# A kernel of four graph layers: the attention of layer 2 transposed by VectorE's blocks and DRAM, and work of VectorE and GpSimd put at other times

## The chip, the core and the metric

The kernel runs on one core of a Trainium2 chip. Its engines are TensorE (PE in the profile, its weight loads are PEld), VectorE (DVE), ScalarE (ACT), GpSimd (POOL) and SyncE (SP), which issues the DMAs. The metric is the device time of one execution in microseconds. All data are float32.

## The reference

`x` has 128 graphs of 128 nodes with 512 features. `adj` is one 128 x 128 matrix for all graphs. Four layers follow one another, each with a residual and a layer norm over the features:

```python
def _L0_gnn_ref(x, adj, weight, bias):
    y = jnp.einsum('nm,bmd->bnd', adj, x)
    return jnp.einsum('bnd,do->bno', y, weight) + bias

def _L1_gnn_ref(s, adjacency, Wq, Wk, Wv):
    q, k, v = s @ Wq.T, s @ Wk.T, s @ Wv.T            # shortened
    rel = adjacency.T[None, :, :] * jnp.einsum('bnd,bmd->bnm', q, k)
    rel = rel / jnp.linalg.norm(rel, axis=2, keepdims=True)
    return jnp.einsum('bnm,bmd->bnd', rel, v)

def _L2_gnn_ref(x, W, a, beta, mask):
    h = jnp.einsum('bnc,cf->bnf', x, W)
    s1, s2 = h @ a[:F_, 0], h @ a[F_:, 0]             # shortened
    e = leaky_relu(s1[:, :, None] + s2[:, None, :], negative_slope=0.2) * mask
    att = jax.nn.softmax(e, axis=2)
    h_prime = jnp.einsum('bij,bjf->bif', att, h)
    return jax.nn.elu(h_prime + beta * h)

def _L3_gnn_ref(x, W1, W2, b):
    A = jnp.einsum('od,bdn->bon', W1, x)
    C = jnp.einsum('od,bdn->bon', W2, x) + b[None, :, None]
    return jnp.max(relu(A[:, :, None, :] + (C - A)[:, :, :, None]), axis=-1)

x = _layernorm(x + _L0_gnn_ref(x, adj, L0_gnn_weight, L0_gnn_bias))
x = _layernorm(x + _L1_gnn_ref(x, adj, L1_gnn_Wq, L1_gnn_Wk, L1_gnn_Wv))
x = _layernorm(x + _L2_gnn_ref(x, L2_gnn_W, L2_gnn_a, L2_gnn_beta, adj))
x = _layernorm(x + _L3_gnn_ref(x, adj, adj, L3_gnn_b))
```

The change is about layer 2. The kernel computes `(att + beta I) x W`: it needs the matrix `att + beta I` transposed, with the nodes that are summed over on the partitions.

## The kernel before

The graphs go through in 32 groups of four (G = 4, NG = 32). Each engine runs its instructions in program order and waits on semaphores for the data. The program order comes from a table of slots: `emit(at, f)` notes a piece of work with its slot, and all pieces are emitted in the order of their slots. A group advances by 28 slots, so slot 65.8 of one group stands beside slot 9.8 of the group two later. The slots set only the order on each engine; nothing holds an instruction back to the time of its slot.

```python
TABLE = dict(
    load=[-20], y=row(0.5, 1), bias=row(1.3, 1), y_sums=row(5.2, 0.5), y_w=row(7, 1, 7),
    ...
    spread=[61.6], leaky=[62.0], weighted=[63.4], greatest=[64.3], exps=[64.4],
    divide=[65.8], turn_att=[68.6], with_beta=[69.0], gather=row(71.5, 1),
    z_sums=row(75.3, 0.5), z_w=row(77, 1, 7), exp=[87.5, 88.5, 90.4, 92.0],
    elu=[87.8, 89.4, 92.8, 93.8], norm2=[95.0], apply2=row(95.7, 0.33),
    widen=[98.7, 100.0, 103.6, 104.6], top=[99.1, 100.4, 104.0, 105.0],
    stats3=[99.8, 101.1, 104.7, 105.7], norm3=[106.2], apply3=row(107, 0.33), store=[108.5],
)
```

The four large products of a group (y_w, m, v, z_w; layer 0's and 2's weights, and layer 1's scores and values) are each split into seven block products with sums of blocks. The sums of the left factor are made by GpSimd (`left_factors`: s1, s2, s3, s4; s2 needs s1, s4 needs s2). The seven products run in the order 1, 2, 6, 5, 7, 3, 4, a slot apart, in accumulators in PSUM: one of two buffers r0 for 1, 6, 7, 4, and a single buffer r12 for first 2 and then 5 and 3. Each is evicted 0.72 slots after it is emitted; in the y product VectorE does all seven evictions. Product 6 takes s2, product 5 s1, product 7 s3, product 3 s4.

```python
r[where] = psum.tile([P, 2, H], FP, tag="r0" if where == 0 else "r12",
                     name=f"r{where}_{name}", bufs=2 if where == 0 else 1)
...
for n, i in enumerate(ORDER):
    emit(at[n], step, i)
    emit(at[n] + 0.72, out, i)
```

The attention of layer 2, for four graphs at once (e is 128 x 4 x 128):

```python
def leaky():                                   # VectorE, twice
    e = work.tile([P, G, P], FP, tag="e", name=f"e_{g}")
    dve.tensor_tensor(e, s["p"]..., s12[g]..., ALU.add)
    dve.scalar_tensor_tensor(e, e, ALPHA, e, op0=ALU.mult, op1=ALU.max)
def weighted():
    pool.tensor_tensor(s["e"], s["e"], adj_b, ALU.mult)
def greatest():
    dve.tensor_reduce(s["nm"], s["e"], AX.X, ALU.max, negate=True)
def exps(i):                                   # ScalarE, four times, with the sums of the rows
    ...
def divide(i):
    rs = small.tile([P, n], FP, tag=f"rs{n}", name=f"rs_{g}_{i}")
    dve.reciprocal(rs, s["sums"][:, i * n : i * n + n])
    e = s["e"][:, i * n : i * n + n, :]
    engine = pool if n == G else dve
    engine.tensor_tensor(e, e, rs[:, :, None].to_broadcast([P, n, P]), ALU.mult)
def turn_att(i):
    for b in range(i * n, i * n + n):
        pe.transpose(s["p"][:, b * P : (b + 1) * P], s["e"][:, b, :], ident)
def with_beta(i):                              # out of PSUM, with beta on the diagonal
    dve.tensor_tensor(s["eT"]..., s["p"]..., beta_b..., ALU.add)
def gather(b):                                 # z = (att + beta I) x, transposed
    pe.matmul(p[:, k * P : (k + 1) * P], x2[g][:, b, k * P : (k + 1) * P], s["eT"][:, b, :], ...)
```

Layer 0's bias is added to the residual by GpSimd, one graph at a time (`biased`), in place. elu is two VectorE operations and the statistics of the norm; layer 3 is one matmul (`widen`) and a maximum (`top`) for each graph. At the end of layer 1 VectorE makes two dot products of each graph with a vector (`dots`) and three tiny operations on their 4 x 2 results (`scale`). Layer 1's x and rel are already transposed without TensorE in most groups: VectorE transposes blocks of 32 x 32, and DMAs move the blocks. The last three groups have tables of their own (LAST).

## Time and profile before

| | before |
|---|---|
| time, median of 3 runs | 2218.94 us (2217.63 to 2219.58) |
| span of the profiled execution | 2214.6 us |
| TensorE granted clock, mean | 0.996 of full speed |
| DVE busy | 1547.9 us (70%) |
| ACT busy | 1102.5 us (50%) |
| POOL busy | 907.7 us (41%) |
| DMA moved | 115.15 MB |
| transposes of e on TensorE | 128, 273 ns each |
| with_beta on VectorE, 128x512 | 31, 674 ns each |
| multiply by 1/sum on GpSimd, 128x512 | 31, 1049 ns each |

The profile is one execution. The page gives each engine's busy time and the chain of work that ended last, followed back from the last instruction to what released each step. A row of the order of time has the start and the duration in us, the engine, the operation, what it writes and reads with the shapes, and the count of instructions merged in the row; in brackets it has the engine's idle time before it and the operation whose end released it. Matmuls overlap, so that a TensorE instruction's duration is longer than its share of the engine's time: the distance of two starts tells more.

### The profile page before, as it was taken

How to read it: one execution, taken by the hardware profiler on the slowest of the kernel's cores; microseconds unless marked ns; L12 is line 12 of the kernel's file. 1: busy time of each engine (PE TensorE's matmuls, PEld its weight loads, DVE VectorE, ACT ScalarE, POOL GpSimd, SP SyncE). 2: the span in 40 equal slices, each digit the busy share in tenths (PEclk: the TensorE clock that was granted, in tenths of full speed). 3: DMA queues.
4: the chain of work that ended last, by engine and by line, in shares of the span. 5: the costliest groups of instructions: out<-in, count | busy, mean ns of one | idle time of the engine just before them, and what ended most of it. 6: DMA issues, size and time to landing. Idle time of an engine off the chain costs nothing.

```text
span 2214.6 us, 31863 instructions
## 1 busy us (share of the span) xinstructions
PE 2170.9 (98%) x11073; PEld 1839.6 (83%) x11073; DVE 1547.9 (70%) x3290; ACT 1102.5 (50%) x2446; POOL 907.7 (41%) x743
## 2 busy tenths in 40 slices
PE   7999999999999999999999999999999999999996
PEld 5788888888888888888888888888888888888873
DVE  4657766767766767776767776767767677667676
ACT  2224445554445554445554445554455554455547
POOL 3334444334444344443344443344443344443321
PEclk9999999999999999999999999999999999999998
DMA  4011222211222211222112222112222112221101
GB/s 167 25 20 29 61 60 62 62 20 49 60 60 63 58 21 52 59 61 62 44 31 56 58 62 63 41 30 59 58 62 63 29 39 62 59 63 44 21 28 57
DMA packets 333295, 115.15 MB, mean 52 GB/s; under 512 B 297424, under 2 KB 297552, under 8 KB 333136
## 3 DMA queue, kind: packets, MB, share of 16 engines
q1 hardware_dynamic: 331936, 110.77, 19.7%
q10 hardware_dynamic: 1200, 2.36, 0.3%
q8 instruction: 88, 1.44, 0.3%
q14 instruction: 71, 0.58, 0.1%
HBM read 39.65 MB, written 33.55 MB: 33 GB/s over the span
## 4 chain that ended last, share of the span: by engine, by line
PE 93%; DVE 3%; ACT 2%; POOL 1%; issue 1%; DMA 0%; ACTq 0%; DVEq 0%; POOLq 0%
PE r_y L26 17%; PE r_v L26 17%; PE r_m L26 17%; PE r_z L26 17%; PE p_z L26 5%; PE p_rel L26 5%; PE p_y L26 5%; PE p_o L26 5%; PE p_a L26 5%; DVE x L26 1%; ACT x L26 1%; DVE st L26 1%; PE p_eT L26 1%; PE p_m L26 1%; PE p_s L26 1%
## 5 line engine op out<-in xcount | busy, mean ns | idle before, releaser
L26 ACT ACTIVATE x<-x,nmean,rstd 128x512 f32<-128x512 f32 x384 | 288.6, 808 | 120.8 <-DVE nmean L26 120.8
L26 DVE BATCH_NORM_STATS2 st<-x 128x6 f32<-128x512 f32 x384 | 263.8, 687 | 8.8
L26 POOL TENSOR_TENSOR x<-x,bias_sb 128x512 f32<-128x512 f32 x128 | 170.1, 1331 | 137.9 <-PE p_y L26 137.5
L26 DVE SCALAR_TENSOR_TENSOR x<-m,x 128x512 f32<-128x512 f32 x128 | 114.4, 894 | 108.5 <-ACT m L26 98.5
L26 POOL TENSOR_TENSOR s_x<-xT 128x512 f32<-128x512 f32 x64 | 82.2, 1285 | 261.1 <-DMA xT<-xB 250.2
L26 ACT COPY c<-r_z 128x512 f32<-128x512 f32 x124 | 71.2, 574 | 223.3 <-PE r_z L26 198.0
L26 ACT COPY yT<-p_y 128x512 f32<-128x512 f32 x128 | 75.1, 586 | 213.6 <-PE p_y L26 213.6
L26 POOL TENSOR_TENSOR rstd<-ve,mhalf 128x4 f32<-128x4 f32 (+1 forms) x99 | 98.5, 995 | 194.1 <-DVE ve L26 188.9
L26 DVE TENSOR_TENSOR x<-r_y,x 128x512 f32<-128x512 f32 x224 | 151.7, 678 | 31.2 <-PE r_y L26 31.0
L26 DVE SCALAR_TENSOR_TENSOR scr<-x,wa 128x512 f32<-128x512 f32 x256 | 161.5, 675 | 0.0
L26 DVE STREAM_TRANSPOSE xB<-x 128x512 f32<-128x512 f32 x120 | 81.2, 696 | 108.7 <-ACT x L26 97.7
L26 PEld LDWEIGHTS p_y<-adjT,x 128*128 128x128 f32 x1024 | 136.9, 196 | 11.2 <-ACT adjT L26 4.8
L26 POOL TENSOR_TENSOR s_z<-zT 128x512 f32<-128x512 f32 x31 | 39.4, 1270 | 255.9 <-ACT zT L26 255.9
L26 PE MATMUL p_y<-adjT,x 128*128 128x128 f32 x1024 | 137.6, 280 | 4.5 <-ACT adjT L26 4.5
L26 PEld LDWEIGHTS p_z<-eT,x 128*128 128x128 f32 x1024 | 134.0, 192 | 7.9 <-issue 1.0
L26 PEld LDWEIGHTS p_rel<-xT,tT 128*128 128x128 f32 x1024 | 134.1, 191 | 7.4 <-DVE tT L26 0.8
L26 DVE TENSOR_REDUCE mx<-p_a 128x1 f32<-128x512 f32 x128 | 88.3, 691 | 69.6 <-PE p_a L26 69.6
L26 PE MATMUL p_a<-x,adjT 128*128 128x512 f32 x256 | 130.8, 596 | 5.8 <-DVE mx L26 4.4
L26 ACT COPY tT<-r_m 128x512 f32<-128x512 f32 x128 | 75.6, 590 | 121.6 <-PE r_m L26 121.6
L26 PE MATMUL p_rel<-xT,tT 128*128 128x128 f32 x1024 | 134.9, 275 | 0.6 <-DVE tT L26 0.6
L26 PE MATMUL p_z<-eT,x 128*128 128x128 f32 x1024 | 134.7, 275 | 0.1
L26 PE MATMUL p_o<-v,relT 128*128 128x512 f32 x256 | 130.4, 593 | 0.3 <-ACT v L26 0.3
(129 smaller groups left out, 5268.6 us busy)
## 6 DMA issues: line engine op xcount, KB each, us to landing
out_dram<-x SPq DMA_DIRECT2D x128, 256.0 KB, 2.5
x<-in_x_dram SPq DMA_DIRECT2D x31, 1024.0 KB, 5.3
xT<-xB SPq DMA_DIRECT2D x480, 64.0 KB, 2.3
relT<-relB SPq DMA_DIRECT2D x512, 16.0 KB, 1.8
w_sb<-in_L_gnn_weight_dram ACTq DMA_DIRECT2D x1, 1024.0 KB, 5.6
x<-in_x_dram SPq DMA_DIRECT2D x4, 256.0 KB, 7.8
wq_sb<-in_L_gnn_Wq_dram SPq DMA_DIRECT2D x1, 1024.0 KB, 12.3
wk_sb<-in_L_gnn_Wk_dram SPq DMA_DIRECT2D x1, 1024.0 KB, 15.1
```

The source lines that it names most:

```text
L26: return lambda *args, **kw: self.tc.keep_in_program_order(op(*args, **kw))
```

## The change

In all groups but the last two, `att + beta I` is transposed without TensorE. VectorE scales each graph's e by 1/sum and adds beta on the diagonal in one operation, four times, and then transposes the 32 x 32 blocks. One DMA writes the result to a DRAM scratch, and four read it back with the blocks in their places. This takes the four transposes from TensorE, the evacuation of their PSUM bank from VectorE, and the multiply from GpSimd. Besides, the order of other work is changed: the biases of graphs 2 and 3 follow layer 0's first two sums, layer 2's softmax starts a little earlier, elu of graphs 0 and 1 comes earlier and of graphs 2 and 3 later, and layer 3's four matmuls stand together.

```diff
+    dram = ctx.enter_context(tc.tile_pool(name="dram", bufs=2, space=bass.MemoryType.DRAM))
...
-        load=[-20], y=row(0.5, 1), bias=row(1.3, 1), y_sums=row(5.2, 0.5), y_w=row(7, 1, 7),
+        load=[-20], y=row(0.5, 1), bias=[4.1, 4.6, 9.1, 9.6],
+        y_sums=[6.8, 7.35, 10.2, 10.75], y_w=row(7, 1, 7),
...
-        spread=[61.6], leaky=[62.0], weighted=[63.4], greatest=[64.3], exps=[64.4],
-        divide=[65.8], turn_att=[68.6], with_beta=[69.0], gather=row(71.5, 1),
-        z_sums=row(75.3, 0.5), z_w=row(77, 1, 7), exp=[87.5, 88.5, 90.4, 92.0],
-        elu=[87.8, 89.4, 92.8, 93.8], norm2=[95.0], apply2=row(95.7, 0.33),
-        widen=[98.7, 100.0, 103.6, 104.6], top=[99.1, 100.4, 104.0, 105.0],
-        stats3=[99.8, 101.1, 104.7, 105.7], norm3=[106.2], apply3=row(107, 0.33), store=[108.5],
+        spread=[61.6], leaky=[61.6], weighted=[62.3], greatest=[63.0], exps=[63.1],
+        divide=[64.2], turn_att=[68.6], with_beta=[69.0], turn_blocks_2=[64.8], move_2=[64.9], gather=row(71.5, 1),
+        z_sums=row(75.3, 0.5), z_w=row(77, 1, 7), exp=[86.0, 87.0, 96.0, 99.6],
+        elu=[86.4, 87.4, 96.8, 100.3], norm2=[101.4], apply2=row(102.4, 0.33),
+        widen=[104.2, 104.9, 105.6, 106.3], top=[104.7, 105.4, 106.1, 106.8],
+        norm3=[107.4], apply3=row(108.4, 0.33), store=[109.8],
...
-    FIRST = {0: dict(turn=row(20.4, 0.3)), 1: dict(y=row(-9.5, 0.3), bias=row(-9.2, 0.3))}
+    FIRST = {0: dict(turn=row(20.4, 0.3)), 1: dict(y=row(-9.5, 0.3))}
...
+        late = g >= NG - 2
...
         def divide(i):
             rs = small.tile([P, n], FP, tag=f"rs{n}", name=f"rs_{g}_{i}")
             dve.reciprocal(rs, s["sums"][:, i * n : i * n + n])
+            if not late:
+                for b in range(G):
+                    e = s["e"][:, b, :]
+                    dve.scalar_tensor_tensor(
+                        e, e, rs[:, b : b + 1], beta_i, op0=ALU.mult, op1=ALU.add
+                    )
+                return
...
+        def turn_blocks():
+            s["eB"] = work.tile([P, Q, G, P // Q], FP, tag="eB", name=f"eB_{g}")
+            dve.transpose(
+                s["eB"].rearrange("p q b u -> p b q u"),
+                s["e"].rearrange("p b (q u) -> p b q u", q=Q),
+            )
+
+        def move():
+            m = P // Q
+            blocks = dram.tile([P, Q, G * m], FP, tag="eB", name=f"eBd_{g}")
+            sync.dma_start(blocks, s["eB"].rearrange("p q b u -> p q (b u)"))
+            eT = work.tile([P, Q, G, m], FP, tag="eT", name=f"eT_{g}")
+            for q in range(Q):
+                sync.dma_start(
+                    eT[q * m : (q + 1) * m].rearrange("p a b u -> p a (b u)"),
+                    blocks.rearrange("(a j) q n -> q j a n", a=Q)[q],
+                )
+            s["eT"] = eT.rearrange("p a b u -> p b a u")
...
-        each(t["turn_att"], turn_att)
-        each(t["with_beta"], with_beta)
+        if late:
+            each(t["turn_att"], turn_att)
+            each(t["with_beta"], with_beta)
+        else:
+            emit(t["turn_blocks_2"][0], turn_blocks)
+            emit(t["move_2"][0], move)
```

## The prediction

> **What bounds the kernel now.** I read the page's totals and its chain first, to see whether one engine sets the end; then TensorE's idle time by releaser, and where it lies; then the order of time within one group of four graphs, engine by engine.

> ```profile
> PE 2170.9 (98%) x11073; PEld 1839.6 (83%) x11073; DVE 1547.9 (70%) x3290; ACT 1102.5 (50%) x2446; POOL 907.7 (41%) x743
> ...
> PE 93%; DVE 3%; ACT 2%; POOL 1%; issue 1%; DMA 0%; ACTq 0%; DVEq 0%; POOLq 0%
> ```

> TensorE is busy for 98% of the span and makes 93% of the chain. Its named waits lie in the first 130 us and the last 105 us; between them there is one, of 0.4 us near 857 us. So a group costs what TensorE takes for it: the r_m product that begins a group recurs every 66.81 us (1117.92 to 1184.73 in the chain). Anything taken from TensorE shortens the kernel, and any new wait of TensorE lengthens it, 30 times over. The other engines have slack on average, but an average says nothing of one moment. So the change must be placed in the order of time.

> The four transposes that the change removes, in the order of time (start, duration, engine, operation, count):

> ```profile
> 1135.48 1.60 PEld L26 LDWEIGHTS r_y<-w_sb,s_y 128*128 128x128 f32 x8
> ...
> 1137.10 0.58 PEld L26 LDWEIGHTS p_eT<-ident,e 128*128 128x128 f32 x4
> ...
> 1137.64 1.60 PEld L26 LDWEIGHTS r_y<-t,yT 128*128 128x128 f32 x8
> ...
> 1139.27 1.70 PEld L26 LDWEIGHTS r_v<-wvT,xT 128*128 128x128 f32 x8
> ```

> They take 0.54 us (1137.10 to 1137.64), but a product behind a 128-wide group starts after 1.62 to 1.63 us instead of the 1.72 of two products in a row, so the net cost is about 0.45 us.

> [...] The trace of before [...] shows that each instruction pays anew:

> ```profile
> 107.87 3.70 POOL L26 TENSOR_TENSOR x<-x,bias_sb 128x512 f32<-128x512 f32 x3
> ...
> 107.91 2.46 DVE L26 SCALAR_TENSOR_TENSOR d<-mv,wa_sum,d 128x4 f32<-128x4 f32 x2
> ...
> 110.47 1.12 DVE L26 TENSOR_TENSOR d<-d,rstd 128x8 f32<-128x8 f32 x1
> ...
> 111.52 0.68 DVE L26 TENSOR_TENSOR tT<-r_m,tT 128x512 f32<-128x512 f32 x1
> ...
> 112.25 2.97 PE L26 MATMUL r_m<-s_x,m_qk 128*128 128x256 f32 x8 [4.39 <-DVE tT L26]
> ```

> Three GpSimd sums run back to back (3.70 us, 1.23 each, not slowed). Beside them three tiny VectorE instructions, some 0.15 to 0.2 us each when alone, take 3.6 us: one gets in after each sum. The eviction behind them (tT) is late, and TensorE waits 4.39 us. [...] behind the 4.39 us the granted clock was 0.62 over 112.2 to 116.0, behind a wait of 2.00 us at 56.70 it stayed 1.00. [...] no line of before has a round trip through DRAM.

> **The change part by part.**

> *TensorE.* In 30 of 32 groups (all but the last two) the four transposes go: 30 x 0.45 = 13.5 us less, if nothing new waits. All else on TensorE is only moved.

> *The DMA route.* The turn is ready some ten slots of the table before its use in gather: one write and four reads, each some 0.65 us to issue (16 DMAs of relT in 10.49 us) and about 2 us to land (1.8 to 2.5 in the page's DMA part): 0.65 + 2.5 + 4 x 0.65 + 2.5, about 8 us. From turn_blocks_2 at slot 8.8 to gather at 15.5 TensorE has some 16 us. An estimate, but hidden with room.

> *VectorE and GpSimd around the softmax: the part that decides.* The scale by 1/sum was one GpSimd multiply. It becomes four VectorE scalar_tensor_tensor of 128x128 with e and beta_i, both in SBUF. GpSimd's order was bias x4, y_sums x4, weighted; it becomes bias x2, weighted, y_sums x2, bias x2, y_sums x2. GpSimd works in order and starts what is ready: behind "weighted" six operations are all ready. So it runs seven in a row. The chain of e in before, to be counted from the first VectorE operation on it (call that moment L, here 1124.17):

> ```profile
> 1124.17 0.68 DVE L26 TENSOR_TENSOR e<-p_s,d 128x512 f32<-128x512 f32 x1
> ...
> 1125.74 1.27 POOL L26 TENSOR_TENSOR e<-e,adj_sb 128x512 f32<-128x512 f32 x1 [0.63 <-DVE e L26]
> ...
> 1127.04 0.69 DVE L26 TENSOR_REDUCE nm<-e 128x4 f32<-128x512 f32 x1 [0.78 <-POOL e L26]
> ...
> 1127.76 0.40 ACT L26 ACTIVATE e<-e,nm 128x128 f32<-128x128 f32 x1 [3.06 <-DVE nm L26]
> ...
> 1129.22 0.19 ACT L26 ACTIVATION_READ_ACCUMULATOR e<-e,nm 128x1 f32 x1
> ```

> The exponentials end at L + 5.24. The reciprocal and a dependent start after it (dependent small operations follow each other by 0.2 us) put the first multiply at about L + 5.47. GpSimd's pace is seen in z_sums, where the second depends on the first and the others do not:

> ```profile
> 1020.64 1.27 POOL L26 TENSOR_TENSOR s_z<-zT 128x512 f32<-128x512 f32 x1 [7.94 <-ACT zT L26]
> ...
> 1021.99 1.27 POOL L26 TENSOR_TENSOR s_z<-s_z,zT 128x512 f32<-128x512 f32 x1
> ...
> 1023.22 1.28 POOL L26 TENSOR_TENSOR zT<-zT 128x512 f32<-128x512 f32 x1
> ...
> 1024.45 1.28 POOL L26 TENSOR_TENSOR s_z<-zT,s_z 128x512 f32<-128x512 f32 x1
> ```

> Weighted starts at L + 1.57, so s1 at 2.80 (+1.23), s2 at 4.16 (+1.36), the third bias at 5.39, then 6.62, 7.85, 9.08. The third bias is thus ahead of the first multiply by 0.08 us. In before a tiny operation waiting behind a sum got in some 1.12 us after the sum's start (1110.15 to about 1111.27). So the multiplies get in near 6.51, 7.75, 9.0 and 10.25. Next in VectorE's order is the eviction of the second y product (slot 8.72 behind divide at 8.2), which ends 0.8 us later, at L + 11.05.

> TensorE needs that eviction, since the r12 accumulator has one buffer and the fourth y product (i = 5) takes it anew:

> ```profile
> 1121.22 0.60 PE L26 MATMUL p_s<-ident,d 128*128 128x128 f32 x4
> ...
> 1127.73 1.89 PE L26 MATMUL r_y<-t,s_y 128*128 128x256 f32 x8
> ...
> 1130.35 1.89 PE L26 MATMUL r_y<-w_sb,s_y 128*128 128x256 f32 x8
> ```

> In the changed kernel leaky stands directly behind spread, so L is the end of p_s, 1121.86 on this scale, and the fourth product would start at 1130.35 = L + 8.49. It has to wait to L + 11.05: 2.55 us. That is below the 4.39 us that lost clock. The third product needs s2 (ready L + 5.45, wanted near L + 5.8): just in time.

> *The rest of the moves.* elu 0 and 1 come earlier, 2 and 3 later, the four widen of layer 3 stand together before attend. I added VectorE's and ScalarE's durations by slot: both engines finish the evictions of v some 0.3 to 1.0 us before TensorE needs the bank again, and the pairs of banks for widen and attend come round in time. I count nothing for this, with up to 0.3 us a group as a risk.

> *The start.* The biases of group 1 go from slot 18.8 to 32.1 and half of group 0's behind its first sums. The waits on GpSimd's s_y (0.68 us) and s_x (2.00 us at 56.70[...]) go, and of the three tiny operations at 107.91 one no longer meets a bias (0.95): about -3 us.

> *Sum.* 30 x (2.55 - 0.45) - 3 = +60 us: 2218.9 + 60 = 2279. I place the prediction a little lower, at 2276, for the first rival.

> **The rivals.** (1) The first multiply is ahead of the third bias. The gap is 0.08 us on sums of a dozen durations, so this is nearly even. Then three waits remain, the stall is 2.55 - 1.24 = 1.3 us, and the time 2219 + 30 x 0.86 - 3 = 2242. (2) The table is meant to leave GpSimd free between 7.9 and 9.1, just where the multiplies stand. If something I don't see holds the third bias back to slot 9.1, nothing collides and only the transposes count: 2219 - 13.5 - 3 = 2202. Against it: the biases' only inputs are the load and the y matmuls, done by then, and in before GpSimd ran each bias as soon as its matmuls ended, whatever the table said. (3) More than I count: elu 2 before the last y eviction delays the v evictions[...], 0.3 to 1 us a group, 2285 to 2305. (4) The DRAM round trip is late and gather waits; that needs it to double, for which no landing of before speaks.

> **Range and chances.** About half of my weight on 2265 to 2290, a quarter on rival 1 (2230 to 2262), 14% on rival 2, a tenth above 2290. A range of 2225 to 2300 holds some 8 in 10. The 2% lines are 2174.6 and 2263.3: faster 0.01, within 0.36, slower 0.63.

> **What would show it.** Right: the multiplies e<-e,rs,beta_i at more than 1 us each, one behind each GpSimd operation; a TensorE wait of r_y on DVE x of 2 to 2.7 us in each of 30 groups, at the fourth y product; a group of about 68.9 us; no wait of p_z on a DMA. Wrong: multiplies of 0.2 to 0.3 us with GpSimd idle beside them and a group of 66.4 us (rival 2); three slow multiplies and 67.7 us (rival 1); TensorE waiting for v or eT instead (rivals 3 and 4).

## The result, and the profile after

The changed kernel takes 2319.90 us (median of 4 runs, 2317.82 to 2320.61) against 2218.28 us before: a ratio of 1.0456 (95% interval 1.0438 to 1.0475), 101.6 us more. The prediction had the direction and the wait, but not the size: 2276 us, and a range that ended at 2300.

The page's totals and its chain, of after:

```profile
PE 2202.7 (95%) x10953; PEld 1854.6 (80%) x10953; DVE 1660.9 (72%) x3410; ACT 1097.0 (47%) x2446; POOL 867.0 (37%) x713
PE 79%; DVE 12%; ACT 4%; issue 2%; POOL 2%; SPq 0%; DMA 0%; ACTq 0%; DVEq 0%; POOLq 0%
```

TensorE's share of the chain fell from 93% to 79%, and VectorE's rose from 3% to 12%: work that lay beside TensorE now lies between its products. VectorE's own busy time rose by 113 us, though the same instructions add only 28 us where the multiplies meet no GpSimd work (1575.5 us in e1, below). TensorE runs 120 transposes fewer and yet is busy for 32 us longer; a row further down shows the main part of it. The page's groups name the two operations (count | busy us, mean ns | idle time before and its releaser):

```profile
L26 PE MATMUL r_y<-w_sb,s_y 128*128 128x256 f32 x512 | 143.7, 430 | 76.6 <-DVE x L26 76.6
...
L26 DVE SCALAR_TENSOR_TENSOR e<-e,rs,beta_i 128x128 f32<-128x128 f32 x120 | 153.7, 1338 | 1.1
```

The multiply by 1/sum takes 1338 ns for 128 elements a partition, and a y product waits 76.6 us in all for VectorE (30 waits). One group in the order of time, of after, with rows left out:

```profile
1100.28 0.60 PE L26 MATMUL p_s<-ident,d 128*128 128x128 f32 x4
...
1100.92 0.69 DVE L26 TENSOR_TENSOR e<-p_s,d 128x512 f32<-128x512 f32 x1 [1.40 <-PE p_s L26]
...
1102.42 1.27 POOL L26 TENSOR_TENSOR e<-e,adj_sb 128x512 f32<-128x512 f32 x1 [9.03 <-DVE e L26]
...
1105.91 0.19 ACT L26 ACTIVATION_READ_ACCUMULATOR e<-e,nm 128x1 f32 x1
1106.13 0.18 DVE L26 RECIPROCAL rs<-sums 128x4 f32<-128x4 f32 x1 [1.06 <-ACT e L26]
1106.23 2.54 POOL L26 TENSOR_TENSOR x<-x,bias_sb 128x512 f32<-128x512 f32 x2
1106.34 5.11 DVE L26 SCALAR_TENSOR_TENSOR e<-e,rs,beta_i 128x128 f32<-128x128 f32 x4
...
1108.73 1.31 POOL L26 TENSOR_TENSOR yT<-yT 128x512 f32<-128x512 f32 x1
1110.00 1.31 POOL L26 TENSOR_TENSOR s_y<-yT,s_y 128x512 f32<-128x512 f32 x1
1111.38 0.68 DVE L26 TENSOR_TENSOR x<-r_y,x 128x512 f32<-128x512 f32 x1
...
1112.11 3.46 PE L26 MATMUL r_y<-w_sb,s_y 128*128 128x256 f32 x8 [2.53 <-DVE x L26]
...
1115.36 1.31 PE L26 MATMUL p_rel<-xT,tT 128*128 128x128 f32 x8
```

The third bias starts at 1106.23, 0.11 us ahead of the first multiply. The four multiplies take 5.11 us beside GpSimd's four operations (1106.23 to 1111.31), one behind each. The eviction behind them ends at 1112.06, and the fourth y product starts then: 2.53 us of wait. This product then takes 3.46 us where eight such instructions take 1.89. Busy time and granted clock in stretches (the number behind the comma is TensorE's busy time, the third from the end is the clock) ahead of, in and behind this wait:

```profile
1107.00:1109.50 2.50, 2.50 (x16) 2.19 (x14) 2.50 (x3) 0.00 (x0) 2.50 (x3) 1.00 0.00 0
1109.50:1112.00 2.50, 0.08 (x1) 0.00 (x0) 2.50 (x4) 0.00 (x0) 1.81 (x2) 1.00 0.00 0
...
1113.50:1115.40 1.90, 1.90 (x6) 1.45 (x6) 0.00 (x0) 1.90 (x4) 0.00 (x0) 0.50 0.35 138
...
1117.00:1119.00 2.00, 2.00 (x14) 1.84 (x13) 0.56 (x1) 0.00 (x0) 0.00 (x0) 1.00 0.14 39
```

So the wait is paid twice: once as idle time, and once more as some 3.4 us at half the clock behind it. The 30 waits have a mean of 2.55 us; behind 19 of them the clock falls to 0.5 for about 3.4 us and 1.71 us of TensorE's full speed are lost, behind the other 11 it stays at 1.00. That is 32.4 us in all. Groups take 69.2 to 69.6 us after a wait without the loss and 70.8 to 71.2 us after one with it, against 66.81 before.

Which of these equal waits lose the clock is in the trace too. The starts of its 22 half-clock stretches lie a whole number of steps of 3.413 us apart (from 1112.47 to 1184.15 it is 21 steps), and all but the last, which runs to the end of the kernel, are 3.413 us long. Cut at these places, the trace has the wait that ends at 479.44 (2.54 us) in two stretches, 0.70 us in the first and 1.85 us in the second, and the clock stays; the wait that ends at 2097.51 (2.54 us) has 2.00 us in the second, and the next stretch has half the clock:

```profile
474.18:477.59 3.41, 2.72 (x17) 2.32 (x16) 3.41 (x4) 0.00 (x0) 3.41 (x4) 1.00 0.00 0
477.59:481.01 3.42, 1.57 (x7) 1.42 (x8) 3.06 (x5) 0.93 (x2) 1.05 (x1) 1.00 0.04 16
481.01:484.42 3.41, 3.41 (x23) 3.15 (x23) 1.02 (x2) 2.52 (x4) 0.00 (x0) 1.00 0.35 119
...
2095.51:2098.92 3.41, 1.41 (x7) 1.25 (x8) 3.21 (x6) 0.77 (x2) 1.20 (x1) 1.00 0.00 0
2098.93:2102.34 3.41, 3.41 (x14) 3.05 (x13) 0.69 (x1) 2.67 (x5) 0.00 (x0) 0.50 0.35 121
```

All 30 waits of after follow this: the 19 with 2.00 us or more in one stretch lose the clock, the 11 with 1.88 or less in either do not. So do all the stretches of before and after, each trace cut at its own half-clock starts: from 20 us on, the clock falls behind each of the 24 full-clock stretches in which TensorE is idle for 2.00 us or more, and behind none of the 1262 with 1.88 us or less.

The way through DRAM is hidden. The issues to landing are 2.0 us for the write and 2.0 us for each read:

```profile
eBd<-eB SPq DMA_DIRECT2D x30, 256.0 KB, 2.0
eT<-eBd SPq DMA_DIRECT2D x120, 64.0 KB, 2.0
```

The reads are issued from 1114.72 on, and gather begins at 1126.04; no wait of TensorE for a DMA appears in the steady state.

### The profile page after: what moved, and what is told of

Its sections match the earlier page's. It is cut to its first block, busy times and chain, and to the rows that moved or that the text cites. A ratio compares the mean times of both kernels' runs of the same rounds, so it can differ in the third digit from the quotient of the medians.

```text
span 2318.4 us, 32156 instructions
## 1 busy us (share of the span) xinstructions
PE 2202.7 (95%) x10953; PEld 1854.6 (80%) x10953; DVE 1660.9 (72%) x3410; ACT 1097.0 (47%) x2446; POOL 867.0 (37%) x713
## 4 chain that ended last, share of the span: by engine, by line
PE 79%; DVE 12%; ACT 4%; issue 2%; POOL 2%; SPq 0%; DMA 0%; ACTq 0%; DVEq 0%; POOLq 0%
PE r_z L26 16%; PE r_v L26 16%; PE r_m L26 14%; PE r_y L26 11%; DVE e L26 7%; PE p_y L26 5%; PE p_z L26 5%; PE p_o L26 4%; PE p_a L26 4%; PE p_rel L26 3%; ACT e L26 2%; DVE x L26 2%; POOL e L26 2%; ACT x L26 1%; DVE nm L26 1%
## 5 line engine op out<-in xcount | busy, mean ns | idle before, releaser
L26 ACT ACTIVATE x<-x,nmean,rstd 128x512 f32<-128x512 f32 x384 | 285.6, 807 | 210.7 <-DVE nmean L26 207.3
L26 DVE BATCH_NORM_STATS2 st<-x 128x6 f32<-128x512 f32 x384 | 263.1, 685 | 8.8
L26 DVE TENSOR_TENSOR x<-r_y,x 128x512 f32<-128x512 f32 x224 | 152.8, 683 | 137.5 <-PE r_y L26 134.0
L26 POOL TENSOR_TENSOR rstd<-ve,mhalf 128x4 f32<-128x4 f32 (+1 forms) x99 | 108.9, 1100 | 335.3 <-DVE ve L26 335.3
L26 PE MATMUL r_y<-w_sb,s_y 128*128 128x256 f32 x512 | 143.7, 430 | 76.6 <-DVE x L26 76.6
L26 POOL TENSOR_TENSOR x<-x,bias_sb 128x512 f32<-128x512 f32 x128 | 172.3, 1358 | 60.4 <-PE p_y L26 60.4
L26 PEld LDWEIGHTS r_y<-w_sb,s_y 128*128 128x128 f32 x512 | 102.4, 210 | 96.0 <-DVE x L26 82.3
L26 ACT COPY yT<-p_y 128x512 f32<-128x512 f32 x128 | 75.1, 587 | 196.8 <-PE p_y L26 196.8
L26 DVE TENSOR_REDUCE mx<-p_a 128x1 f32<-128x512 f32 x128 | 88.3, 691 | 105.1 <-PE p_a L26 102.4
L26 DVE SCALAR_TENSOR_TENSOR scr<-x,wa 128x512 f32<-128x512 f32 x256 | 162.3, 679 | 0.0
L26 PEld LDWEIGHTS p_rel<-xT,tT 128*128 128x128 f32 x1024 | 147.8, 208 | 9.8 <-DVE tT L26 0.8
L26 DVE SCALAR_TENSOR_TENSOR e<-e,rs,beta_i 128x128 f32<-128x128 f32 x120 | 153.7, 1338 | 1.1
L26 ACT ACTIVATE x<-x,mean,r 128x512 f32<-128x512 f32 x128 | 97.1, 808 | 111.2 <-DVE mean L26 111.2
L26 POOL TENSOR_TENSOR e<-e,adj_sb 128x512 f32<-128x512 f32 x32 | 40.7, 1273 | 285.4 <-DVE e L26 280.2
L26 PE MATMUL p_rel<-xT,tT 128*128 128x128 f32 x1024 | 146.6, 290 | 0.6 <-DVE tT L26 0.6
L26 ACT COPY tT<-r_m 128x512 f32<-128x512 f32 x128 | 75.6, 590 | 149.8 <-PE r_m L26 149.8
L26 PEld LDWEIGHTS p_y<-adjT,x 128*128 128x128 f32 x1024 | 135.7, 195 | 11.7 <-ACT adjT L26 5.3
L26 POOL TENSOR_TENSOR rn<-n,mhalf 128x4 f32<-128x4 f32 x32 | 32.6, 1017 | 292.9 <-ACT sq L26 292.9
L26 PEld LDWEIGHTS p_z<-eT,x 128*128 128x128 f32 x1024 | 135.0, 193 | 7.9 <-issue 1.2
L26 PE MATMUL p_y<-adjT,x 128*128 128x128 f32 x1024 | 136.4, 278 | 5.0 <-ACT adjT L26 5.0
L26 PE MATMUL p_z<-eT,x 128*128 128x128 f32 x1024 | 135.9, 276 | 0.1
L26 PE MATMUL p_a<-x,adjT 128*128 128x512 f32 x256 | 126.3, 597 | 5.8 <-DVE mx L26 4.4
```

Source lines behind the costliest of these rows:

```text
L26: return lambda *args, **kw: self.tc.keep_in_program_order(op(*args, **kw))
```

## The experiments

Two theories stood against the one of GpSimd's sums beside the multiplies and the clock behind the wait. Rival A: the multiplies are slow in themselves. Rival B: the moved work or the way through DRAM costs the time.

**e1: GpSimd's sums at their slots of before.** GpSimd then does four biases, three sums, "weighted" and s4. The order in the expectation, with s4 ahead of "weighted", is not quite that of the table (6.7 against 6.3); s4 is over before the multiplies all the same.

```diff
-        load=[-20], y=row(0.5, 1), bias=[4.1, 4.6, 9.1, 9.6],
-        y_sums=[6.8, 7.35, 10.2, 10.75], y_w=row(7, 1, 7),
+        load=[-20], y=row(0.5, 1), bias=row(1.3, 1),
+        y_sums=row(5.2, 0.5), y_w=row(7, 1, 7),
```

> The changed kernel with GpSimd's biases and first sums at their slots of before (bias x4, y_sums x4, then weighted), so that GpSimd has nothing to run while the four multiplies run. Theory [...]: the multiplies e<-e,rs,beta_i fall from 1.3 us to about 0.3 us each, the wait of r_y on DVE x (2.54 us, 30 times) is gone, the clock stays at 0.996, a group takes about 66.4 us and the kernel 2200 to 2208 us, below both kernels. Rival A (the multiplies are slow in themselves, through their scalar operand or in-place write): they stay at 1.3 us and the time near 2320. Rival B (the way through DRAM or the moved elu and layer 3 cost the time): above 2260, with other waits.

Measured: 2206.72 us, ratio to before 0.995 (0.9935 to 0.9965), clock 0.995. The order of time of e1 around the multiplies:

```profile
1117.42 1.28 POOL L26 TENSOR_TENSOR e<-e,adj_sb 128x512 f32<-128x512 f32 x1 [0.63 <-DVE e L26]
1118.66 1.27 POOL L26 TENSOR_TENSOR s_y<-yT,s_y 128x512 f32<-128x512 f32 x1
...
1121.35 1.14 DVE L26 SCALAR_TENSOR_TENSOR e<-e,rs,beta_i 128x128 f32<-128x128 f32 x4
...
1122.41 0.68 DVE L26 TENSOR_TENSOR x<-r_y,x 128x512 f32<-128x512 f32 x1
```

GpSimd is done at 1119.93, and the same four multiplies take 1.14 us instead of 5.11 (347 ns each). No wait of TensorE has a name from 130 to 2030 us. GpSimd's order alone makes 113 us of difference. Rival A falls, and so does B in the form that the new way must be slow.

**e2: the eviction ahead of the multiplies.** GpSimd's order is left as changed, and so are the collisions; the block transposes go behind the next eviction.

```diff
-        divide=[64.2], ... turn_blocks_2=[64.8], move_2=[64.9], ...
+        divide=[64.74], ... turn_blocks_2=[65.74], move_2=[65.76], ...
```

> The changed kernel with divide directly behind the eviction of the second y product instead of ahead of it, and the block transposes behind the eviction of the third. GpSimd's order is left as changed. Theory: the multiplies still take 1.3 us each, since GpSimd still runs beside them, but TensorE no longer waits at the fourth product; the fifth may wait 0.2 to 1 us for the eviction behind the multiplies, too short to lose the clock. 2203 to 2235 us. Rival A (what counts is how late e is finished, not which eviction stands behind it): the time stays above 2280.

Measured: 2213.97 us, ratio 0.998 (0.9973 to 0.9987), clock 0.994. The multiplies still take 1.35 us in the median (1.20 in the mean), and the named waits are gone; the fifth product starts some 0.25 us behind its place, without a named wait. So the multiplies cost time only through what stands behind them: the same slow instructions, one place later, are worth 106 us.

**e3: work in place of the wait.**

```diff
+        def fill():
+            p = bank(f"p_fill_{g}")
+            for _ in range(5):
+                pe.matmul(p[:, :H], adjT, w2_sb[:, 0, :H], start=True, stop=True)
+
+        if g >= 2:
+            emit(t["y_w"][3] - 0.05, fill)
```

> The changed kernel with five useless 128x128 by 256 matmuls (about 2.16 us, into a spare PSUM bank that nobody reads) ahead of the fourth y product from group 2 on: they fill TensorE's wait with work and change nothing else. Theory (the wait costs more than its length because TensorE's clock halves for 3.4 us behind 19 of 30 waits): the fourth product still starts when its bank is free, the clock goes back to about 0.996, and the kernel gets faster by 19 x 1.7 = 32 us and a little for the shorter refill: 2278 to 2290 us. Rival (the low clock has another cause than the idle time): the clock stays at 0.98 and the time at 2320 or above.

Measured: 2288.65 us, ratio to before 1.0316 (1.0301 to 1.0332), clock 0.995. TensorE's order of time in e3:

```profile
959.00 2.32 PE L26 MATMUL p_fill<-w_sb,adjT 128*128 128x256 f32 x10
961.72 1.99 PE L26 MATMUL r_y<-w_sb,s_y 128*128 128x256 f32 x8 [0.40 <-DVE x L26]
963.55 1.05 PE L26 MATMUL p_rel<-xT,tT 128*128 128x128 f32 x8
```

(Each of the five matmuls is two instructions in the trace.) The product still waits for its bank, 0.40 us behind the fill, and then runs at full speed. Five useless matmuls in each of 30 groups make the kernel 31 us faster, and the groups take 69.2 to 69.6 us, as those of after without a loss do: this is the sum of the clock's losses, measured by itself. None of the 30 waits has a loss of clock.

**e4: three multiplies.** It leaves work out: graph 3 of each group is neither scaled nor given beta.

```diff
-                for b in range(G):
+                for b in range(G - 1):
```

> The changed kernel with the multiply of the fourth graph left out (its attention is not scaled and has no beta: work left out). Theory: each multiply costs one GpSimd operation of 1.27 us, so the wait falls from 2.54 to about 1.27 us, which is too short for the clock to fall; 2319.9 - 30 x 1.27 - 32 = 2250 us, range 2243 to 2258, clock 0.996. Rival (the clock loss goes in proportion to the wait): about 2266 us. Rival A (multiplies slow in themselves): same wait of 1.27, cannot be told apart here.

Measured: 2248.81 us, ratio 1.014 (1.0125 to 1.0155), clock 0.995. The 30 waits are 1.28 us in the mean, and behind none of them the clock falls. One multiply less takes 1.27 us from each wait and the whole loss of clock; it is worth 71 us, of which its own wait is 38.

**e5: the moves alone.** All groups turn the attention as before, in the changed order.

```diff
-        late = g >= NG - 2
+        late = True
```

> The changed table and order in full, but all groups turn the attention as before: GpSimd multiplies by 1/sum, TensorE transposes, VectorE adds beta out of PSUM. Theory: the moves by themselves cost nothing in the steady state and take some 3 us from the start: 2213 to 2220 us, no wait of r_y on DVE x. Rival B (the moves cost): above 2225 us.

Measured: 2217.22 us against 2218.13, ratio 0.9995 (0.9987 to 1.0004). In sum the moves cost nothing. Groups take 66.8 to 67.2 us, 0.13 more in the mean of the 28 middle groups than in before (66.96 against 66.83), some 4 us that the start gains back: the v product of the third group begins at 199.25 us instead of 203.46.

**e6: the new way alone, in the order of before.** The diff puts `turn_blocks_2=[66.9], move_2=[67.0]` into the table of before and takes the functions of the change over unaltered.

> The kernel before with the new way of turning the attention alone: the multiplies at before's slot of divide (GpSimd idle there), block transposes and DMAs at 66.9 and 67.0, all else at before's slots. Theory: multiplies of 0.3 us, transposes of TensorE saved, 2218.3 - 13.5 = 2205 us, up to 2215 where VectorE, fuller in these slots than in the changed kernel, evicts late. Rival B (the way through DRAM costs): gather waits for a DMA, above 2225 us.

Measured: 2231.44 us, ratio 1.0059 (1.0042 to 1.0076): slower than before, and in the range of rival B. But not for B's reason: the multiplies are fast (347 ns), and no product waits for a DMA. VectorE and TensorE in e6, in the order of time:

```profile
1141.43 1.14 DVE L26 SCALAR_TENSOR_TENSOR e<-e,rs,beta_i 128x128 f32<-128x128 f32 x4
...
1142.49 0.69 DVE L26 TENSOR_TENSOR x<-r_y,x 128x512 f32<-128x512 f32 x1
1143.09 0.71 DVE L26 STREAM_TRANSPOSE eB<-e 128x512 f32<-128x512 f32 x1
...
1144.98 0.16 DVE L26 SCALAR_TENSOR_TENSOR nmean<-mv,rstd 128x4 f32<-128x4 f32 x1 [1.13 <-POOL rstd L26]
1145.06 0.69 DVE L26 TENSOR_TENSOR x<-r_y,x 128x512 f32<-128x512 f32 x1
...
1145.80 1.99 PE L26 MATMUL r_y<-t,yT 128*128 128x256 f32 x8 [0.52 <-DVE x L26]
```

In before's order two elu and the norm of layer 2 stand in these slots too. The multiplies and the block transpose push that norm back, VectorE waits 1.13 us for its power on GpSimd, and TensorE waits 0.52 us for the eviction behind it, in 29 groups. The product starts 0.76 us behind its place and its neighbours 0.05 and 0.10 us behind theirs, so that the groups take 67.28 us, 0.91 more than the 66.37 of e7 below. The difference to e1, 25 us, is the other moves taken together, which cost nothing alone: the new way needs them. The rows point to elu and the norm; which of the moves it takes was not tried singly.

**e7: e1, with layer 3's normalization behind a z eviction on ScalarE.** In e1 half of the groups take 66.6 to 66.7 us instead of 66.37. The order of time of e1 shows one:

```profile
1028.36 1.27 POOL L26 TENSOR_TENSOR s_x<-xT 128x512 f32<-128x512 f32 x1 [1.52 <-PE r_z L26]
...
1028.47 1.17 DVE L26 TENSOR_TENSOR mean<-mean,r 128x4 f32<-128x4 f32 x1
...
1029.68 0.81 ACT L26 ACTIVATE x<-x,mean,r 128x512 f32<-128x512 f32 x1 [4.05 <-DVE mean L26]
...
1030.40 0.56 ACT L26 COPY c<-r_z 128x512 f32<-128x512 f32 x1
...
1031.11 1.96 PE L26 MATMUL r_z<-w_sb,s_z 128*128 128x256 f32 x8
```

It is the same collision, in small: a VectorE multiply of four elements, 1.17 us here and 0.15 to 0.17 where no GpSimd operation is beside it in before, waits behind a sum of GpSimd, ScalarE waits for it, and the eviction of c behind that comes late for TensorE: the r_z product starts 1.10 us behind the start of p_o (1030.01), in e7 0.86 us.

```diff
-        norm3=[107.4], apply3=row(108.4, 0.33), store=[109.8],
+        norm3=[107.4], apply3=row(108.8, 0.33), store=[110.2],
```

> The kernel of e1 (sums as before) with layer 3's normalization on ScalarE (apply3) at 24.8 instead of 24.4, behind the eviction of a z product at 24.72 instead of ahead of it. In e1 the groups take 66.37 to 66.7 us: where it is more, that eviction stands behind apply3, which waits for a tiny VectorE multiply that GpSimd's sums hold up by 1.2 us. Theory: all groups at 66.37, on average 0.17 us a group less, 2206.7 - 5 = 2201 to 2204 us, ratio to before about 0.993. Rival (the 0.3 us come from elsewhere): 2206 to 2208 us.

Measured: 2202.14 us, ratio to before 0.993 (0.9917 to 0.9942), and every group from 600 to 1700 us takes 66.37 or 66.38 us. This is the fastest version: 16.7 us below before, near the 16.5 us that the prediction gave the transposes and the start together.

**e8: a fifth multiply.** Into a scratch, behind the four.

```diff
+                x = work.tile([P, P], FP, tag="extra", name=f"extra_{g}", bufs=2)
+                dve.scalar_tensor_tensor(
+                    x, s["e"][:, 0, :], rs[:, 0:1], beta_i, op0=ALU.mult, op1=ALU.add
+                )
```

> The changed kernel with a fifth multiply of the same form in each group, into a scratch that nobody reads. GpSimd has only four operations left to run beside them, so if the price is one GpSimd operation for each multiply, the fifth finds GpSimd idle and costs only some 0.2 to 0.35 us: a wait of 2.75 to 2.9 us, 2327 to 2345 us with a few more losses of clock. Rival A (each such multiply costs 1.3 us by itself): a wait of 3.8 us, 2319.9 + 38 and more losses of clock, 2360 to 2380 us.

Measured: 2333.94 us, ratio to before 1.0521 (1.0505 to 1.0537). The order of time of e8 has both prices of one instruction side by side:

```profile
1116.03 1.31 POOL L26 TENSOR_TENSOR s_y<-yT,s_y 128x512 f32<-128x512 f32 x1
1117.41 0.34 DVE L26 SCALAR_TENSOR_TENSOR extra<-e,rs,beta_i 128x128 f32<-128x128 f32 x1
1117.68 0.68 DVE L26 TENSOR_TENSOR x<-r_y,x 128x512 f32<-128x512 f32 x1
```

The fifth takes 340 ns, since GpSimd's last sum is over; the four take 1347 ns in the median. The wait grows by 0.27 us to 2.82, and the clock is lost behind 22 of 30 instead of 19. So a multiply pays only where it meets a GpSimd operation, one for each.

## Why the prediction was right or wrong

**Right: the collision, and its arithmetic.** The step from the three tiny operations at 107.91 held: one multiply gets in behind each GpSimd operation, 1338 ns in the mean beside operations of 1.27 to 1.31 us. In the trace of before, the same kind of operation on four times the elements, but with wa in PSUM, is not held up by a GpSimd sum beside it:

```profile
1108.68 1.27 POOL L26 TENSOR_TENSOR s_x<-xT,s_x 128x512 f32<-128x512 f32 x1
...
1108.73 0.68 DVE L26 SCALAR_TENSOR_TENSOR scr<-x,wa 128x512 f32<-128x512 f32 x1
...
1109.34 0.68 DVE L26 SCALAR_TENSOR_TENSOR scr<-x,wa 128x512 f32<-128x512 f32 x1
```

None of the 256 in after takes more than 0.69 us. The multiplies have e and beta_i in SBUF. The runs show the price and this difference, not what is behind them. The first rival (the multiply comes first) was near: the third bias led by 0.11 us, where 0.08 was worked out. The eviction was put at L + 11.05 and came at 1112.06 - 1100.92 = L + 11.14. The wait was put at 2.55 us and was 2.55 in the mean of 30. Rival 2, that something holds the third bias back, did not come true.

**Right: the transposes.** The net 0.45 us a group is what e7 has: 66.81 - 66.37 = 0.44.

**Right: DRAM and the moves.** The round trip lies beside other work, and e5 shows no price of the moves in sum. What was missed there is that the new way depends on them (e6).

**Wrong: "That is below the 4.39 us that lost clock."** This was the step that failed. Between a wait of 2.00 us without loss and one of 4.39 us with it, the prediction put 2.55 on the safe side, and entered the wait into the sum with its bare length. Behind 19 of 30 waits TensorE ran at half speed for some 3.4 us. This term, entered as zero, is 32.4 us by the granted clock and 31 us by e3. Rival 3 allowed 0.3 to 1 us a group for more than was counted; this term alone is 1.08 in the mean.

So the length of a wait was the wrong thing to compare; its place counts as well. Of the 4.39 us in before only 2.55 lay in the 3.41 us ahead of the fall of the clock at 113.11, and that the 2.00 us at 56.70 stayed at 1.00 was luck: they lay in two stretches, 0.39 and 1.62 us. The same wait in e6, 2.01 us, lay in one, and half the clock followed. Before:

```profile
51.67:55.08 3.41, 3.03 (x15) 2.32 (x13) 3.41 (x4) 0.82 (x2) 3.33 (x3) 1.00 0.00 0
55.08:58.50 3.42, 1.80 (x8) 1.62 (x9) 3.42 (x6) 0.00 (x0) 3.42 (x3) 1.00 0.00 0
58.50:61.91 3.41, 3.41 (x17) 3.00 (x17) 0.38 (x2) 1.17 (x2) 3.33 (x3) 1.00 0.02 5
```

e6:

```profile
53.95:57.36 3.41, 1.40 (x7) 0.92 (x6) 3.41 (x6) 0.00 (x0) 3.33 (x3) 1.00 0.00 0
57.36:60.77 3.41, 3.41 (x10) 2.70 (x9) 1.30 (x2) 0.59 (x1) 3.41 (x3) 0.50 0.00 0
```

With a limit of 1.94 us, between the 1.88 and 2.00 of before and after, an estimate of the missing term can be made: a wait of 2.55 us at a random place has less than the limit in both of its stretches in (2 x 1.94 - 2.55) / 3.41 = 39% of cases, so that some 18 of 30 are hit, against 19 measured; for the 2.82 us of e8 it gives 21, against 22 measured.

**Too small: the price of a wait.** Behind a wait the products also refill: in the groups of e4 the fourth product starts 1.43 us behind its place for a wait of 1.27, and its successor starts 0.10 us later than usual. That is about 0.26 us a group, 8 us in all, which the prediction left out.

**The sum again.** 30 x (2.55 + 0.26 - 0.44) + 32.4 - 3 = 100.5 us; 101.6 were measured. The terms of the prediction were +60 without 32 of clock and 8 of refill. That the sum comes so near is in part luck: the -3 of the start was not measured by itself, and some 4 us that e7 removes (0.14 us a group, 66.51 in the mean of e1's 28 middle groups against 66.37) are not in it.

## What to carry to other kernels

Where VectorE operations with both inputs in SBUF meet GpSimd sums, count instructions and not elements: beside sums of 1.27 to 1.31 us a multiply of 128x128 took 1338 ns instead of 347, and an operation of 128x8 1.12 us instead of 0.17, so splitting one operation in four can cost four waits, as it did here, and a cure is to choose what stands in GpSimd's order at that moment, or to let no eviction stand behind it. A wait that the tensor engine meets in every round has to be charged with more than its length: here 2.55 us cost 3.9 in the mean, of which 1.1 was the clock. Whether the clock was lost hung on how much of the wait fell into one 3.41 us stretch (2.00 us or more of it lost the clock, 1.88 or less did not), so a single wait that went unpunished does not show that its length is safe.
